# Selective scans in one kernel of four layers: x of the next task fetched a block ahead, five tiles for delta * x, other landing times

## The chip, the cores and the metric

The program runs on one NeuronCore of a Trainium2 chip. Its time is the device time of one execution in microseconds; the figure compared is the median over several runs. The profile is of one execution.

## The reference

Four layers follow each other on an input of 4 images of 64 x 64 points and 128 channels. Layers 0 and 1 are selective scans with projections, convolutions and norms around them; layer 2 is a gate over the edges to nine neighbours and layer 3 is attention in a 7 x 7 window. Nearly all of the time, and all that the change touches, lies in layers 0 and 1. Their core, here of layer 1 (256 channels, 16 states a channel, 4 directions; layer 0 has 128 channels):

```python
xs = jnp.stack([x0, x1, x0[..., ::-1], x1[..., ::-1]], axis=1)   # rows, columns, and both reversed
x_dbl = jnp.einsum('bkdl,kcd->bkcl', xs, x_proj_w)
dts, Bs, Cs = jnp.split(x_dbl, [R, R + N], axis=2)
dts = jnp.einsum('bkrl,kdr->bkdl', dts, dt_w)
delta = jax.nn.softplus(dts + dt_b[None, :, :, None])
A = -jnp.exp(A_log).reshape(K, DI, N)

def step(h, t):
    x_t, d_t, B_t, C_t = t
    h = jnp.exp(d_t[..., None] * A) * h + (d_t * x_t)[..., None] * B_t[:, :, None, :]
    return (h, jnp.einsum('bkdn,bkn->bkd', h, C_t))
...
ys = jnp.moveaxis(ys_l, 0, -1) + Ds.reshape(K, DI)[None, :, :, None] * xs
```

The sequence has 4096 steps.

## The kernel before

**Tasks, steps, units.** A task is one image, one layer and one tile of 128 channels: 4 tasks of layer 0 (tasks 0 to 3), then 8 of layer 1 (tasks 4 to 11, two for each image). The two tasks of one image share x and the projections of the first of them; in the code `t.first` names that first task. A task has 16 steps: 4 directions by 4 pieces of 1024 positions. A step has 16 units; a unit is 8 channels x 16 states = 128 rows by 1024 positions. So there are 12 x 256 = 3072 units, and `Scans.run` emits them in one loop over `u`. A group of 16 units is called a block here.

**One unit.** SP loads `dub`, the 8 rows of delta * x, each for its 16 states, from DRAM (`load`, 512 KB). POOL multiplies it by B into `dbu` (`times_b`). PE spreads three bfloat16 parts of delta (`dp`) over 128 rows into a PSUM tile `da`, and ACT takes the exponential of it in place (`decay`). DVE scans `da` and `dbu` into `da`, copies the last column to `state`, and multiplies by C into `hc` (`scan`). Every four units PE adds up the states with the constant `gather` (`add_up`). In iteration u the loop emits scan(u), times_b(u+3), decay(u+2) and load(u+6). There are 4 dub tiles, 3 dbu, 2 da.

**Preparation.** Each block needs a preparation (`prepare`), begun 22 units ahead (`AHEAD`): projection matmuls of x into `xd`, a store of it to `xdd` in DRAM, a delta projection from `xd` and `dtw`, softplus of it over ACT and POOL, the product delta * x on POOL (`low`), its store to DRAM (`dud`), three bfloat16 parts of delta (`parts`), loads of B and C repeated over channels (`repB`, `repC`), and 12 loads of `dp`. A second task of an image loads `xd` back from `xdd` instead of projecting. Each `yield` in `prepare` ends a piece. One unit of the loop is `rest` of its block: at rest 0 the old preparation is run to its end and the next one is started.

**x.** `fetch` loads the x of a task (`xc`, one tile for each 128 channels, single buffered) in 4 chunks of 512 KB a tile. It is called where the first step's preparation starts; the first chunk of each tile goes out at once, the others one a unit.

**The planner.** All instructions are put in order by hand when the program is built. `Plan` keeps an estimate of when PE, ACT and POOL are free; a piece is taken into a unit if it `fits`, that is if its start, not earlier than the time its data is taken to have landed, plus its usual cost, is before the end of the unit plus some slack. `LANDING`, `FOUR_LANDING` and `ROWS_LANDING` are those landing times. Stores are posted and issued when they are due. Where fewer than `rest - 2` pieces are out, a piece is taken without a look at the estimate.

**The side work.** Everything else of layers 0 and 1 (projections, convolutions, norms, the MLP) is cut into pieces as well and put between the units (`between`), paced by what is left until the next deadline. `last` holds the unit by which the side work that feeds a scan group must be out; past it, all of it is taken at once.

All engines work in order, and SP issues nearly all transfers. So an instruction that waits holds back what stands behind it on its engine: a projection of x on PE holds the decay products, a dub load on SP holds every later transfer.

Of the kernel before, what the change touches and what calls it, by code (L numbers as in the profile page):

```python
# [17 lines left out]
P = 128  # L18
# [26 lines left out]
class Consts:  # L45


    def __init__(self, tc, pool, d_gather, d_spread):
        nc = tc.nc

        self.gather = pool.tile([P, 4, 32], F32, name="gather")
        nc.sync.dma_start(out=self.gather, in_=d_gather)

        self.spread = pool.tile([96, 4, P], BF16, name="spread")
        with tc.tile_pool(name="spread32", bufs=1) as tmp:
            spread = tmp.tile([96, 4, P], F32, name="spread32")
            nc.sync.dma_start(out=spread, in_=d_spread)
            nc.vector.tensor_copy(self.spread, spread)
        self.ident = pool.tile([P, P], F32, name="ident")
        make_identity(nc, self.ident)  # L60
        self.ones128 = pool.tile([P, P], F32, name="ones128")
        nc.vector.memset(self.ones128, 1.0 / 128.0)
        self.ones256 = pool.tile([P, P], F32, name="ones256")
        nc.vector.memset(self.ones256, 1.0 / 256.0)
        self.cen128 = pool.tile([P, P], F32, name="cen128")
        nc.vector.tensor_sub(self.cen128, self.ident, self.ones128)
        self.cen256 = pool.tile([P, P], F32, name="cen256")
        nc.vector.tensor_sub(self.cen256, self.ident, self.ones256)
        self.neg256 = pool.tile([P, P], F32, name="neg256")
        nc.vector.memset(self.neg256, -1.0 / 256.0)  # L70
        self.eps = pool.tile([P, 1], F32, name="eps")
        nc.vector.memset(self.eps, EPS)

# [33 lines left out]
UNIT = 3.85  # L107
USUAL = dict(PE=2.1, ACT=0.7, TAB=3.3, POOL=1.3)
SLACK = dict(PE=1.2, ACT=2.2, POOL=3.0)
LANDING = 6.0  # L110
FOUR_LANDING = 12.0
ROWS_LANDING = 12.0


class Plan:
# [84 lines left out]
class ScanWeights:  # L200


    def __init__(self, tc, pool, layer, d_xp, d_dtw, d_av):
        nc = tc.nc
        self.layer, self.nct, self.rank = layer, TILES[layer], RANKS[layer]
        nct, rank = self.nct, self.rank
        self.xp = pool.tile([P, nct, ND, H], F32, name=f"xp{layer}")
        nc.sync.dma_start(out=self.xp, in_=d_xp)
        self.dtw = pool.tile([H + rank, ND, nct * P], F32, name=f"dtw{layer}")
        for i in range(HALVES):  # L210
            nc.sync.dma_start(out=self.dtw[i * H : i * H + rank], in_=d_dtw)
        n = ND * nct * NG
        av = pool.tile([P, n + 2 * ND * nct], F32, name=f"av{layer}")
        nc.sync.dma_start(out=av, in_=d_av)
        self.a = av[:, 0:n]
        nc.scalar.activation(self.a, self.a, AF.Exp)
        nc.vector.tensor_scalar_mul(self.a, self.a, -1.0)
        self.dtb = av[:, n : n + ND * nct].rearrange("p (k t) -> p k t", k=ND)
        ds = av[:, n + ND * nct :].rearrange("p (t k) -> p t k", t=nct)
        self.dsum = pool.tile([P, nct], F32, name=f"dsum{layer}")  # L220
        nc.vector.reduce_sum(self.dsum, ds, axis=AX.X)


class Task:


    def __init__(self, W, b, ct, first, xcd, yd):
        self.W, self.b, self.ct, self.xcd, self.yd = W, b, ct, xcd, yd
        self.first = first
        self.xc, self.xdd, self.prepared, self.states, self.y = [], {}, {}, {}, None  # L230
        self.steps = [
            (k, c) for k in range(ND) for c in (reversed(range(NSTEP)) if k >= 2 else range(NSTEP))
        ]
# [6 lines left out]
class Scans:  # L240
# [33 lines left out]
    def fetch(self, t):  # L274

        if t.first:
            t.xc = t.first.xc
            return
        t.xc = [self.pool.tile([P, L], F32, name=f"xc{i}", tag=f"xc{i}", bufs=1) for i in range(t.W.nct)]
        for c in range(NSTEP):  # L280
            for i, xc in enumerate(t.xc):
                cols = slice(c * TS, (c + 1) * TS)
                self.nc.sync.dma_start(out=xc[:, cols], in_=t.xcd[i][:, cols])
                yield

    def prepare(self, t, step):
# [8 lines left out]
        if t.first is None:  # L295
            xdd = t.xdd[step] = self.dram.tile(
                [rows, TS], F32, name="xdd", tag=f"xdd{W.layer}", bufs=(4, 2 * len(t.steps))[W.layer]
            )
            ps = self.bank()
            for ti in range(W.nct):  # L300
                for i in range(HALVES):
                    nc.tensor.matmul(
                        image(ps[i * H : (i + 1) * H, :]),
                        W.xp[:, ti, k, :],
                        self.view(t.xc[ti], k, c, i, HALVES),
                        start=ti == 0,
                        stop=ti == W.nct - 1,
                    )
            yield "ACT"
            nc.scalar.copy(xd, ps)  # L310

            def store_xd():
                for i in range(HALVES):
                    nc.sync.dma_start(out=xdd[:, half(i)], in_=xd[i * H : i * H + rows, :])

            post("prep", store_xd)
            ready = max(self.plan.done, self.plan.now) + LANDING
            yield "PE"
        else:
            xdd, ready = t.first.xdd[step], begin  # L320
            for i in range(HALVES):
                nc.sync.dma_start(out=xd[i * H : i * H + R, :], in_=xdd[0:R, half(i)])
            yield "PE", self.plan.now + LANDING
# [33 lines left out]
        nc.scalar.copy(parts[:, 0, :], delta)  # L357
        nc.gpsimd.tensor_mul(image(low), image(delta), self.view(t.xc[t.ct], k, c, 0, 1))
        yield "POOL"
        dud = out["du"] = self.dram.tile([P, TS], F32, name="dud", tag="dud", bufs=3)  # L360
        post("prep", lambda: nc.sync.dma_start(out=dud, in_=low))
        nc.gpsimd.tensor_sub(delta, delta, parts[:, 0, :])
# [24 lines left out]

    def load(self, u):
        t, step, jj, j, g = self.unit(u)
        dud = t.prepared[step]["du"]  # L390
        dub = self.live["dub", u] = self.tile("dub", 4)
        src = bass.AP(dud.tensor, dud.offset + 8 * g * TS, [[0, NS], [TS, 8], [1, TS]])
        self.nc.sync.dma_start(out=dub, in_=src)

# [53 lines left out]
    def add_up(self, u, i):  # L448

        for v in range(u - 3, u + 1):  # L450
            t, step, jj, j, g = self.unit(v)
            cols = self.half(i)
            self.nc.tensor.matmul(  # L453
                self.live["yps"][32 * j : 32 * j + 32, cols],
                self.C.gather[:, jj, :],
                self.live["hc", v][:, cols],
                start=False,
                stop=jj == 3,
            )
            if i == HALVES - 1:  # L460
                del self.live["hc", v]
# [15 lines left out]
    def run(self, between):  # L477

        total = NU * len(self.tasks)
        first = self.tasks[0]  # L480
        for _ in self.fetch(first):
            pass
        for _ in self.prepare(first, 0):
            pass
        self.plan.start()
        pieces, fetch = Lane(self.plan, iter(())), iter(())
        for u in range(-6, total):
            if u >= 0:
                self.scan(u)
            if u >= 2:  # L490
# [16 lines left out]
                self.plan.flush("prep", "rep")  # L507
            if rest == 0 and 0 < ahead < total // NG:
                n, step = divmod(ahead, NU // NG)
                if step == 0:  # L510
                    self.plan.flush("side")
                    fetch = self.fetch(self.tasks[n])
                    for _ in range(self.tasks[n].W.nct):
                        next(fetch, None)
                pieces = Lane(self.plan, self.prepare(self.tasks[n], step))
            next(fetch, None)
            while (pieces.count < rest - 2 or pieces.fits()) and pieces.step():
                pass
            if u >= 0:
                n, i = divmod(u, NU)  # L520
                if self.later:
                    self.later.pop(0)()
                between(n, i)
            if 0 <= u + 6 < total:
                self.load(u + 6)
        self.add_up(total - 1, 1)
        self.keep(total - 1)
        while self.later:
# [3 lines left out]
class Side:  # L532
# [218 lines left out]
    def norm(self, xs, out, then):  # L751
# [20 lines left out]
        ps = self.bank()  # L772
        for i, sq in enumerate(sqs):
            nc.tensor.matmul(
                ps, C.ones128 if len(xs) == 1 else C.ones256, sq, start=i == 0, stop=i == len(xs) - 1
            )
        yield "ACT"
        rs = sqs[0]
        nc.scalar.activation(rs, ps, AF.Ln, bias=C.eps)
        nc.scalar.activation(rs, rs, AF.Exp, scale=-0.5)  # L780
        yield "POOL"
        for d in ds:
# [255 lines left out]
def scan_layers(tc, C, nb, x_in, d0, s0, d1, s1, out):  # L1038

    nc = tc.nc  # L1040
    with ExitStack() as es:
# [17 lines left out]
                group.append(n)  # L1059
        scans = Scans(tc, C, pool, psum, dram, tasks, plan)  # L1060

        last = {g: group.index(g) * NU - AHEAD - 1 for g in range(1, len(groups))}
        last[len(groups)] = NU * len(tasks) - 16
        lane, current, credit = None, None, 0.0

# [703 lines left out]
def selectors():  # L1769

    gather = np.zeros((P, 4, 32), np.float32)
    for p in range(P):
        for jj in range(4):
            gather[p, jj, 8 * jj + p % 8] = 1.0
    spread = np.tile(np.transpose(gather, (2, 1, 0)), (3, 1, 1))
    return gather, np.ascontiguousarray(spread)


# [143 lines left out]
```

## Time and profile before

| | us |
|---|---|
| time of the runs: median (lowest to highest, 3 runs) | 14386.92 (14371.29 to 14389.15) |
| the profiled execution: its own time | 14397.46 |
| the profiled execution: its span, first to last instruction | 14395.7 |
| ahead of the first scan | 203.5 |
| first scan to the end of the last product | 11519.8 |
| rest of layer 1, layers 2 and 3 | 2672.4 |
| a scan on DVE, with and without a carried state | 2.350, 2.291 |
| the product by C on DVE, the state copy | 1.218, 0.158 |
| the product by B on POOL | 2.356 |
| the exponential on ACT | 1.089 |

The mean granted TensorE clock of this execution is 0.716; in the scans it is 0.68. The three largest busy shares of the span are DVE 87%, PE 72% and POOL 69%; the DMA queue of the program took 70.8% of 16 DMA engines. These are means over stages with different limits, so the stage of the scans has to be looked at by itself: its busy times, and, for each engine, what ended its waits. A line such as "DVE da L418 <- ACT da L408: 392.7, 312, 11.9" says that DVE's instructions at line 418 sat idle for 392.7 us in total, 312 times, 11.9 us at the longest, until ACT's instruction at line 408 released them. Line 98 is the planner's wrapper, through which all PE, ACT and POOL instructions pass, so there the tiles tell them apart: `mp` is the PSUM tile of the preparation, `ms` that of the side work.

The profile's page gives no landing times of these transfers. Where one is told below, it is worked out from the trace: from the issue to the last update of the transfer's semaphore before that semaphore's next use.

### The profile page before, as it was taken

The page shows a single profiled execution, that of the slowest core. Times are in us where ns is not written, and L with a number is a line of the kernel's source. Part 1 is how long each engine was busy: PE and PEld are TensorE (multiplying, and loading weights), DVE is VectorE, ACT ScalarE, POOL GpSimd, SP SyncE. Part 2 cuts the span into 40 slices and gives each one's busy share as a digit, 9 for nine tenths or more (in the row PEclk, how much of TensorE's full clock was granted, in tenths as well). Part 3 has the DMA queues.
Part 4 walks back from the last instruction along what each step waited for, and adds up shares of the span by engine and source line. Part 5 has one row for each costly group of instructions (what it writes and reads, how often), then busy time and mean ns, then how long its engine had stood idle before and what let it go on. Part 6 is the DMA issues. An engine that isn't in the chain of part 4 may idle for free. (4 is left out here: it accounts for less than half of the span.)

```text
span 14395.7 us, 123898 instructions
## 1 busy us (share of the span) xinstructions
PE 10393.2 (72%) x36216; PEld 2642.4 (18%) x36216; DVE 12507.0 (87%) x10488; ACT 7832.1 (54%) x9246; POOL 9888.4 (69%) x4606
## 2 busy tenths in 40 slices
PE   5777777777767777677776777767677766666999
PEld 1111111111111111111111111111111112113555
DVE  4998899989999999999998999999999954775666
ACT  3666456545655465555655555555555546553555
POOL 4777788778877788778887888888888853551000
PEclk7666666666677666677666777667776668777999
DMA  6888888888889888988889878778877841443000
GB/s 162 215 214 218 204 207 220 217 220 210 206 225 221 201 215 207 224 206 207 211 205 220 207 194 205 194 195 211 200 194 198 198 128 52 104 107 76 13 13 8
DMA packets 893467, 2567.49 MB, mean 178 GB/s; under 512 B 144375, under 2 KB 166143, under 8 KB 884599
## 3 DMA queue, kind: packets, MB, share of 16 engines
q1 hardware_dynamic: 892791, 2559.57, 70.8%
q8 instruction: 291, 4.77, 0.1%
q14 instruction: 385, 3.15, 0.1%
HBM read 2135.71 MB, written 272.37 MB: 167 GB/s over the span
## 5 line engine op out<-in xcount | busy, mean ns | idle before, releaser
L398 POOL TENSOR_TENSOR dbu<-dub,repB 128x1024 f32<-128x1024 f32 x3072 | 7195.6, 2356 | 1647.1 <-DVE da L418 859.1
L418 DVE TENSOR_TENSOR_SCAN da<-da,state,dbu 128x1024 f32<-128x1024 f32 x2304 | 5415.1, 2350 | 375.9 <-ACT da L408 287.9
L408 ACT ACTIVATE da<-da,av 128x1024 f32<-128x1024 f32 x3072 | 3342.0, 1089 | 3780.0 <-PE da L406 3736.2
L406 PE MATMUL da<-dp,spread 96*128 96x512 bf16 x6144 | 2603.8, 518 | 2953.2 <-DVE hc L430 2924.1
L430 DVE TENSOR_TENSOR hc<-da,repC 128x1024 f32<-128x1024 f32 x3072 | 3740.5, 1218 | 40.5 <-PE ms L98 0.5
L453 PE MATMUL yps<-hc,gather 128*32 128x512 f32 x12288 | 2376.5, 856 | 2.3 <-DVE hc L430 2.3
L418 DVE TENSOR_TENSOR_SCAN da<-da,dbu 128x1024 f32<-128x1024 f32 x768 | 1759.1, 2291 | 322.5 <-POOL dbu L398 212.4
L406 PEld LDWEIGHTS <-spread 96*128 96x128 bf16 x6144 | 474.3, 107 | 6513.8 <-DVE hc L430 4152.9
L98 ACT ACT_TABLE_LOAD x600 | 769.8, 1283 | 85.8 <-DMA xcd<-o 67.7
L98 PE MATMUL ms<-d,wts 128*128 128x512 f32 (+3 forms) x900 | 704.2, 905 | 141.8 <-POOL d L98 103.3
L98 POOL TENSOR_TENSOR delta<-delta,low 128x1024 f32<-128x1024 f32 x192 | 452.2, 2355 | 458.3 <-ACT low L98 457.9
L98 PE MATMUL mp<-xd,dtw 8*128 8x512 f32 (+1 forms) x768 | 674.5, 972 | 49.1 <-DMA xd<-xdd 31.2
L98 ACT CAST parts<-delta 128x1024 bf16<-128x1024 f32 x384 | 399.8, 1041 | 299.4 <-POOL delta L98 294.1
L446 PE MATMUL yps<-y,ident 128*128 128x512 f32 x576 | 528.9, 1013 | 2.9 <-ACT y L471 2.6
L453 PEld LDWEIGHTS yps<-hc,gather 128*32 128x32 f32 x12288 | 284.5, 128 | 1207.6 <-issue 1201.8
L98 POOL TENSOR_TENSOR low<-delta,xc 128x1024 f32<-128x1024 f32 x192 | 501.6, 2613 | 2.2
L1702 ACT ACTIVATE s<-s,nmax 128x512 f32<-128x512 f32 x512 | 366.1, 717 | 251.4 <-DVE nmax L1699 246.4
L1330 ACT ACTIVATE hid<-hid,relb 128x1024 f32<-128x1024 f32 x288 | 323.0, 1146 | 259.5 <-DVE hid L1325 259.3
L98 ACT ACTIVATE low<-mp,av 128x512 f32<-128x512 f32 x384 | 263.8, 687 | 365.6 <-PE mp L98 365.4
L1432 POOL TENSOR_TENSOR acc<-acc,part 128x1024 f32<-128x1024 f32 x120 | 315.1, 2633 | 211.7 <-DVE part L1426 154.6
L98 PE MATMUL ms<-pad,diag 96*32 96x504 f32 (+1 forms) x2304 | 423.7, 830 | 50.6 <-DMA pad<-xid 30.0
L1691 PE MATMUL sps<-k,q 32*128 32x512 f32 x1024 | 437.0, 652 | 21.2 <-DVE s L1698 21.2
(275 smaller groups left out, 11419.1 us busy)
## 6 DMA issues: line engine op xcount, KB each, us to landing
dub<-dud SPq DMA_DIRECT2D x3072, 512.0 KB
dp<-parts SPq DMA_DIRECT2D x2304, 64.0 KB
repB<-xdd SPq DMA_DIRECT2D x192, 512.0 KB
repC<-xdd SPq DMA_DIRECT2D x192, 512.0 KB
dud<-low SPq DMA_DIRECT2D x192, 512.0 KB
spread<-gd SPq DMA_DIRECT2D x72, 1024.0 KB
pad<-xid SPq DMA_DIRECT2D x192, 256.0 KB
szd<-o SPq DMA_DIRECT2D x96, 256.0 KB
```

The lines of the kernel that those rows point to most:

```text
L98: return call(*args, **kw)
L398: self.nc.gpsimd.tensor_mul(dbu, self.live.pop(("dub", u)), t.prepared[step]["B"])
L406: self.nc.tensor.matmul(da[:, cols], self.C.spread[:, jj, :], dp[:, j, cols], start=True, stop=True)
L408: self.nc.scalar.activation(da, da, AF.Exp, scale=t.W.a[:, at : at + 1])
L418: nc.vector.tensor_tensor_scan(da[:, way], da[:, way], dbu[:, way], 0.0 if step % NSTEP == 0 else t.states[step - 1][:, g : g + 1], ALU.mu ...
L430: nc.vector.tensor_mul(hc, da, t.prepared[step]["C"])
L446: self.nc.tensor.matmul(out, lhs, self.view(rhs, k, c, i, HALVES), start=True, stop=False)
L453: self.nc.tensor.matmul(self.live["yps"][32 * j : 32 * j + 32, cols], self.C.gather[:, jj, :], self.live["hc", v][:, cols], start=False, s ...
L1330: nc.scalar.activation(hid, hid, AF.Gelu, bias=self.relb[:, m, t : t + 1])
L1432: (nc.vector if alone and pair else nc.gpsimd).tensor_add(acc, acc, part)
L1691: nc.tensor.matmul(sps[:, h, :], q[ch, toks], k[ch, keys], start=True, stop=True)
L1702: nc.scalar.activation(s[:, i, :], s[:, i, :], AF.Exp, bias=nmax[:, h : h + 1], accum_out=total[:, h : h + 1],)
```

## The change

- `fetch` of the next task's x begins one block earlier: once the last preparation of the task before has emitted its product with the old x (`x_done`). One chunk goes out a unit. It flushes the side work's posted stores first. Where `x_done` isn't set in time, the fetch begins where it did.
- dub has five tiles and load(u+7) in place of four and load(u+6); the loop begins at -7. Posted stores of the preparation are flushed ahead of a block's first load.
- `LANDING` is 8 in place of 6, `ROWS_LANDING` 14 in place of 12.
- The projection matmuls of layer 1 (two tiles of x) are two pieces in place of one; pieces are forced up to `rest - 1` in place of `rest - 2`.
- Deadlines in `last` are 16 units sooner.
- Room in SBUF: `xp` and `dtw` of the two layers share one tile, loaded where the layer's first task is prepared; `gather` is a 56-column tile with four overlapping windows; `ones256` is gone and its factor moves into the scale of the logarithm.

```diff
@@ Consts
-        self.gather = pool.tile([P, 4, 32], F32, name="gather")
-        nc.sync.dma_start(out=self.gather, in_=d_gather)
+        gather = pool.tile([P, 56], F32, name="gather")
+        nc.sync.dma_start(out=gather, in_=d_gather)
+        self.gather = [gather[:, 24 - 8 * jj : 56 - 8 * jj] for jj in range(4)]
...
-        self.ones256 = pool.tile([P, P], F32, name="ones256")
-        nc.vector.memset(self.ones256, 1.0 / 256.0)
...
-LANDING = 6.0
+LANDING = 8.0
 FOUR_LANDING = 12.0
-ROWS_LANDING = 12.0
+ROWS_LANDING = 14.0
@@ ScanWeights
-        self.xp = pool.tile([P, nct, ND, H], F32, name=f"xp{layer}")
-        nc.sync.dma_start(out=self.xp, in_=d_xp)
-        self.dtw = pool.tile([H + rank, ND, nct * P], F32, name=f"dtw{layer}")
-        for i in range(HALVES):
-            nc.sync.dma_start(out=self.dtw[i * H : i * H + rank], in_=d_dtw)
+        self.nc, self.pool, self.d_xp, self.d_dtw = nc, pool, d_xp, d_dtw
...
+    def load(self):
+        nct, most = self.nct, max(TILES)
+        tile = self.pool.tile([P, most * ND * (H + P)], F32, name="xpdt", tag="xpdt", bufs=1)
+        self.xp = tile[:, 0 : nct * ND * H].rearrange("p (t k h) -> p t k h", t=nct, k=ND)
+        at = most * ND * H
+        self.dtw = tile[:, at : at + ND * nct * P].rearrange("p (k c) -> p k c", k=ND)
+        self.nc.sync.dma_start(out=self.xp, in_=self.d_xp)
+        for i in range(HALVES):
+            self.nc.sync.dma_start(out=self.dtw[i * H : i * H + self.rank], in_=self.d_dtw)
@@ Scans.fetch
         if t.first:
             t.xc = t.first.xc
             return
+        self.plan.flush("side")
@@ Scans.prepare
-            yield "ACT"
+                yield "PE" if ti + 1 < W.nct else "ACT"
             nc.scalar.copy(xd, ps)
...
         nc.gpsimd.tensor_mul(image(low), image(delta), self.view(t.xc[t.ct], k, c, 0, 1))
         yield "POOL"
+        t.x_done = step == len(t.steps) - 1
@@ Scans.load
         t, step, jj, j, g = self.unit(u)
+        if g == 0:
+            self.plan.flush("prep")
         dud = t.prepared[step]["du"]
-        dub = self.live["dub", u] = self.tile("dub", 4)
+        dub = self.live["dub", u] = self.tile("dub", 5)
@@ Scans.run
         first = self.tasks[0]
+        first.W.load()
...
-        for u in range(-6, total):
+        for u in range(-7, total):
...
-                if step == 0:
-                    self.plan.flush("side")
-                    fetch = self.fetch(self.tasks[n])
+                if step == 0 and self.tasks[n].W is not self.tasks[n - 1].W:
+                    self.tasks[n].W.load()
+                if step == 0 and fetched < n:
+                    fetch, fetched = self.fetch(self.tasks[n]), n
                     for _ in range(self.tasks[n].W.nct):
                         next(fetch, None)
                 pieces = Lane(self.plan, self.prepare(self.tasks[n], step))
+
+            n, step = divmod(ahead + 1, NU // NG)
+            if step == 0 and fetched < n < len(self.tasks) and self.tasks[n - 1].x_done:
+                fetch, fetched = self.fetch(self.tasks[n]), n
             next(fetch, None)
-            while (pieces.count < rest - 2 or pieces.fits()) and pieces.step():
+            while (pieces.count < rest - 1 or pieces.fits()) and pieces.step():
                 pass
...
-            if 0 <= u + 6 < total:
-                self.load(u + 6)
+            if 0 <= u + 7 < total:
+                self.load(u + 7)
@@ Side.norm
-                ps, C.ones128 if len(xs) == 1 else C.ones256, sq, start=i == 0, stop=i == len(xs) - 1
+                ps, C.ones128, sq, start=i == 0, stop=i == len(xs) - 1
...
-        nc.scalar.activation(rs, ps, AF.Ln, bias=C.eps)
+        nc.scalar.activation(rs, ps, AF.Ln, bias=C.eps, scale=1.0 / len(xs))
@@ scan_layers
-        last = {g: group.index(g) * NU - AHEAD - 1 for g in range(1, len(groups))}
+        last = {g: group.index(g) * NU - AHEAD - NG - 1 for g in range(1, len(groups))}
```

More of the change, by code (lines that the diff above doesn't have):

```diff
@@ L67, in __init__ @@
         self.cen256 = pool.tile([P, P], F32, name="cen256")
-        nc.vector.tensor_sub(self.cen256, self.ident, self.ones256)
         self.neg256 = pool.tile([P, P], F32, name="neg256")
         nc.vector.memset(self.neg256, -1.0 / 256.0)
+        nc.vector.tensor_add(self.cen256, self.ident, self.neg256)
         self.eps = pool.tile([P, 1], F32, name="eps")
@@ L229, in __init__ @@
         self.first = first
+        self.x_done = False
         self.xc, self.xdd, self.prepared, self.states, self.y = [], {}, {}, {}, None
@@ L454, in add_up @@
                 self.live["yps"][32 * j : 32 * j + 32, cols],
-                self.C.gather[:, jj, :],
+                self.C.gather[jj],
                 self.live["hc", v][:, cols],
@@ L485, in run @@
         self.plan.start()
-        pieces, fetch = Lane(self.plan, iter(())), iter(())
-        for u in range(-6, total):
+        pieces, fetch, fetched = Lane(self.plan, iter(())), iter(()), 0
+        for u in range(-7, total):
             if u >= 0:
@@ L1775, in selectors @@
     spread = np.tile(np.transpose(gather, (2, 1, 0)), (3, 1, 1))
+    gather = np.concatenate([gather[:, 3, :], np.zeros((P, 24), np.float32)], 1)
     return gather, np.ascontiguousarray(spread)
```

## The prediction

> **What bounds the kernel now.** I read the page first for the busy times and the slices, then one window from the first scan to the end of the last, then the waits of each engine inside it, then the timeline around single stalls.
>
> ```profile
> DVE  4998899989999999999998999999999954775666
> ...
> DMA  6888888888889888988889878778877841443000
> ```
> ```profile
> 203.50:11723.30 11519.80, 8226.40 (x25364) 1702.62 (x25364) 10888.92 (x8460) 6362.61 (x6667) 9292.30 (x4270) 0.68 0.83 208
> ```
>
> The reader is to see that VectorE is nearly full for 32 of 40 slices. The window's columns are its length, then busy time and count of PE, PEld, DVE, ACT and POOL, then clock, DMA share and GB/s. DVE is busy 10888.9 of 11519.8 us (94.5%), and 3072 units share the window: 3.75 us a unit, of which 3.54 are work. Nothing in the diff shortens a scan, a state copy or a product on DVE, so all that can be won here is DVE's idle time, 11519.8 - 10888.9 = 630.9 us. The other 203.5 us ahead and 2672.4 us behind hold no part of the change that matters.
>
> ```profile
> DVE da L418 <- ACT da L408: 392.7, 312, 11.9
> DVE da L418 <- POOL dbu L398: 291.2, 66, 187.1
> ```
> ```profile
> POOL dbu L398 <- DMA dub<-dud: 712.5, 293, 20.0
> ```
> ```profile
> PE mp L98 <- DMA xc<-xcd: 55.5, 7, 12.6
> PE ms L98 <- DMA pad<-ld: 50.2, 8, 9.8
> PE mp L98 <- DMA xd<-xdd: 31.2, 6, 11.8
> ...
> PE ms L98 <- DMA x<-yd: 17.2, 4, 6.3
> PE ms L98 <- DMA x<-in_x_dram: 14.7, 2, 7.7
> ```
> ```profile
> ACT L98 <- DMA xcd<-o: 67.7, 19, 11.9
> ACT sq L98 <- DMA xid<-sq: 37.9, 21, 6.5
> ```
>
> These are waits between 200 and 11730 us: who waited for whom, sum, times, longest. 187.1 us of the second line is the wait for the very first unit, so DVE's named idle time in the scans is 392.7 + 104.1 and some 10 of smaller lines, 506 us; the remaining 125 us are gaps under 150 ns. The engines in front of DVE in turn stand for transfers. I went through the scans with a gap over 150 ns and asked of each whether PE, ACT or POOL had waited for a transfer in the 3.5 us ahead of the gap or inside it: that holds for 262 of the 506 us. By transfer: dub 77.6 us (38 gaps), xc 51.3 (7), pad 40.0 (8), xd 30.7 (6), the side work's x 32.1 (7), stores that ACT waited for 29.4 (10). The other 244 us are ACT and PE being late without a transfer; the change does not touch their causes.
>
> **The x fetch.** The start of task 3 shows the case:
>
> ```profile
> 3061.83 0.29 PEld L98 LDWEIGHTS mp<-xc,xp 128*64 128x64 f32 x4 [13.54 <-DMA xc<-xcd]
> 3061.83 1.98 PE L98 MATMUL mp<-xc,xp 128*64 128x512 f32 x4 [12.63 <-DMA xc<-xcd]
> ...
> 3066.00 2.36 DVE L418 TENSOR_TENSOR_SCAN da<-da,state,dbu 128x1024 f32<-128x1024 f32 x1 [11.89 <-ACT da L408]
> ```
>
> The first projection is issued in the same unit as its chunk of x and stands on PE in front of the next decay product, behind which stand ACT's exponential and the scan. At the seven starts that fetch (tasks 1, 2, 3, 4, 6, 8, 10) DVE lost 11.89 + 6.67 + 11.89 + 6.43 + 7.74 + 7.28 + 4.92 = 56.8 us. After the change the first chunk goes out when the last product with the old x has been issued. The store of that product (dud) stands a median 26.9 us ahead of the next block's first dub issue in this trace, so the fetch starts some 6 units (23 us) before the block ends; by the semaphore updates an xc chunk lands in a median 8.5 us, at most 15.7. So the wait is gone at six starts. At task 4 it is replaced: the scan weights of layer 1 are now loaded there (3 transfers, an earlier such issue takes 0.33 to 0.43 us) directly ahead of the projection that needs them. The trace has them only at the start of the program; bounds are 0 and the 11.89 us of the worst x start. I take the 6.4 of this same start. **Gain 56.8 - 6.4 = 50 us**; bounds 45 and 57. The moved step issues the same 48 chunks on SP. Behind chunk 0 on SP stand the next dub loads: it waits for POOL to have read the old x, at most one sum and one product (2.36 + 2.61 = 5.0 us). A dub lands a median 4.7 us before it is used, and 3.75 more with the fifth tile, so this is hidden; uncovered it costs 7 x 5.0 = 35 us. I charge 5.
>
> **The fifth dub tile.** Load u+7 into five tiles waits for the same product (u+2) as load u+6 into four. So SP is held as before, but each load has a unit, 3.75 us, more. The 38 gaps lie in 26 clusters; cutting each cluster's sum by 3.6 us (a unit's work) leaves 14.9 of 77.6. **Gain 63 us**; bounds 0 (the transfers are bandwidth, and depth buys nothing) and 78. DMA share is 0.83 over the stage and 0.77 to 0.89 by task, so lateness comes in bursts, which depth covers: I stay near the upper end. The first load of a block now comes a unit sooner behind the store it reads: that store had landed at least 4.8 us before, so 1.0 us is left.
>
> [...] The trace has a median landing of 6.1 us, 10.3 at the ninetieth percentile and 19.7 at most, and the 293 waits above: I go by the trace.
>
> **Landing times.** The planner holds a piece until its transfer is due. Measured by semaphore updates: pad of the convolutions median 12.1 (ninetieth percentile 16.5) against a constant of 12; xcd stores 8.7, none under 7.0, against 6; xd 4.4 (6.2). Pieces go out once a unit, so 2 us more delay one by 2 us on average. Pad: 8 gaps x 2 = 16; side x: 7 x 2 = 14; stores: 10 x 2 = 20. xd is deterministic: ready 6 us after its issue fits at the second unit (3.85 + 1.2 + 3.85 covers 6 + 2.1), ready after 8 only at the third, so a whole unit: 6 x 3.75 = 22. **Sum 72**, of 132 that stand there; bounds 0 and 132. A later piece still can collide elsewhere, so I take 60.
>
> **What costs or gives nothing.** The split of the four projection matmuls into two pieces, and pieces forced a unit sooner (dud goes out a median 7.2 units ahead of its block's end, and the old rule forces it only 3 ahead, so few are forced): 0, bounds -10 and +15. The side work's deadline 16 units sooner: the last xcd stores of the four layer-1 groups come at units 753, 1192, 1612 and 2024 against new deadlines of 985, 1497, 2009 and 2521, so 232 to 497 units are to spare. Gather window, the removed constant, the scale inside the logarithm: same instructions, one 0.17 us memset less. Weights of layer 0 loaded at u=-7 instead of at 4.2 us: 3 issues of some 0.4 us ahead of an x fetch that waits for the side work's last store anyway.
>
> **Sum.** 50 - 5 + 63 + 60 = 168 us off the profiled execution's 14397.5 us (span 14395.7): 14229. The median of the runs, 14386.9, is 10.5 lower, which would give 14219. I say **14225**.
>
> **The rivals.**
> *Depth and landing give nothing* (0.17): dub lateness is bandwidth, and delayed pieces land on other units; x alone remains. For it: DMA share 0.9 in slices. Against: tasks 8 to 11 run at 0.77 to 0.81 and still show 3 to 5 us of gap a block at times. Time 14397 - 45 = 14350, faster by 0.3%.
> *No difference* (0.09): the stall of x returns as a later one, since chunks (512 KB a unit beside dub's 512 KB, 280 GB/s against 226 at best in any 400 us) now crowd the dp loads of the last block; 14360 to 14415. Against: the same crowding stood at the block's start before.
> *The change does not do what it says* is in this too: if the last product is issued only in the last unit, the fetch falls back to the old place.
> *Slower* (0.11): held pieces put the side work behind. Place: the last side group, whose final store comes at unit 3047 against a deadline of 3056, where all that is left is issued at once. Price: about 1.3 us of DVE idle a piece (a table load takes 1283 ns, an ACT piece 0.69 us). It decides from 168 / 1.3 = 130 pieces left, of 290; with 200 left the time is 14397 - 168 + 260 = 14490. Against: the pace is computed anew each unit from what is left, and credit lets several pieces go in one unit.
>
> **How the numbers follow.** Forecast 0.63: its own range is 14397 less 95 (x 45, half of dub's 60, a third of the landings' 60) to 262 (all that stands behind transfers), 14135 to 14302. A measurement here tells 0.2%, 29 us, from no change. Faster: forecast 0.63 and 0.17 of the first rival; same 0.09; slower 0.11. The range goes from 14110 (all 262, and 25 of the untouched 244) to 14375, which takes in the first rival and part of the second; what is left out is the slower case, the rest of the second and some 0.03 below.
>
> **What would show it.** Right: no PE wait for xc inside the scans save at task 4 (there for the weights); POOL's wait for dub well under 712 us, DVE's for POOL near 40 (without the first 187); PE waits for pad, xd and x and ACT waits for xcd and xid stores about half; DVE's busy time in the scans unchanged at 10889 and the stage near 11350 us; the 2672 us behind unchanged. Wrong: POOL still waits some 700 us for dub, or DVE's wait for ACT stays at 390, or grows in the last 60 units.

## The result, and the profile after

The changed kernel takes 14310.4 us (median of 4 runs, 14285.4 to 14319.5) against 14388.0 us before (4 runs): ratio 0.9946, 95% interval 0.9929 to 0.9963. That is 78 us less, where 163 were forecast. The profiled execution has a span of 14299.9 us, 95.8 less than before's; all but 0.6 of it is in the stage of the scans. (Lines of the kernel have moved by some ten: after the change, line 97 is the planner's wrapper, 410 the product by B, 420 the exponential, 430 the scan and 405 the load of dub; `xpdt` is the tile of scan weights that the two layers share.)

The window of the scans, after; columns as before (length, busy time and count of PE, PEld, DVE, ACT and POOL, clock, DMA share, GB/s):

```profile
202.70:11627.30 11424.60, 8187.62 (x25364) 1684.33 (x25364) 10879.78 (x8459) 6357.95 (x6665) 9285.10 (x4270) 0.69 0.85 210
```

The stage is 95.2 us shorter at nearly the same busy time of DVE (10879.8 against 10888.9), and 14299.9 - 11627.3 = 2672.6 us follow it, as before. So 86 of the 95 us are idle time of DVE, 544.8 us in place of 630.9. Lines picked from the waits of DVE, POOL, PE and ACT, after, from 200 to 11640 us, and from those of SP, from 200 to 11620 us:

```profile
DVE da L430 <- ACT da L420: 374.2, 309, 11.8
DVE da L430 <- POOL dbu L410: 232.8, 43, 186.3
```
```profile
POOL dbu L410 <- DMA dub<-dud: 367.5, 132, 18.3
```
```profile
PE ms L97 <- DMA pad<-ld: 35.8, 4, 11.8
PE ms L97 <- DMA x<-in_x_dram: 23.0, 2, 15.0
PE mp L97 <- DMA xpdt<-in_w_dram: 12.0, 1, 12.0
PE ms L97 <- DMA x<-yd: 11.9, 3, 4.6
...
PE mp L97 <- DMA xd<-xdd: 0.4, 1, 0.4
```
```profile
ACT L97 <- DMA xcd<-o: 100.0, 24, 11.0
```
```profile
SPq L405 <- DMA dud<-low: 128.9, 30, 14.4
```

The reader is to see that most of what was announced happened at its own place. PE no longer waits for xc, nor for xd (31.2 us before); POOL waits half as long for dub (712.5), and DVE for POOL 46.5 us without the first unit (104.1). But ACT's wait for the stores of the depthwise convolution went up from 67.7 to 100.0 us, PE's waits for the side work's x (31.9 us before, 34.9 after) were not halved, and DVE's wait for ACT only fell from 392.7 to 374.2. The last line is new: at 30 block starts SP stands at the load of dub until the store of delta * x (dud) that it reads has landed; before the change that was one wait of 0.7 us.

To compare kernels I sorted every gap of over 150 ns ahead of a scan by one rule: to dub where POOL ended it; else to the transfer for which PE or ACT had waited longest since the previous exponential; else to no transfer. (This counts all gaps that POOL ended, so dub stands at 112.0 us before, where the prediction's narrower rule gave 77.6.) All in us, from one profiled execution each:

| | all gaps | dub | xc | weights | xd | pad | side x | stores | no transfer |
|---|---|---|---|---|---|---|---|---|---|
| before | 511.4 | 112.0 | 51.3 | 0 | 14.2 | 38.5 | 32.9 | 40.7 | 213.9 |
| after | 425.7 | 47.2 | 0 | 11.0 | 0.7 | 36.6 | 32.6 | 85.9 | 201.3 |

"Side x" is the x that the side work loads. Gaps of under 150 ns and small kinds are in the first column alone. Where PE and ACT had both waited, the rule must choose: before the change some 18 us could stand under stores or under xd.

### The profile page after: what moved, and what is told of

It is laid out like the page before. It is cut to its first block, busy times and chain, and to the rows that moved or that the text cites. A ratio compares the mean times of both kernels' runs of the same rounds, so it can differ in the third digit from the quotient of the medians.

```text
span 14299.9 us, 124251 instructions
## 1 busy us (share of the span) xinstructions
PE 10354.0 (72%) x36216; PEld 2624.8 (18%) x36216; DVE 12498.6 (87%) x10487; ACT 7828.5 (55%) x9246; POOL 9880.8 (69%) x4606
## 5 line engine op out<-in xcount | busy, mean ns | idle before, releaser
L418 PE MATMUL da<-dp,spread 96*128 96x512 bf16 x6144 | 2568.6, 512 | 2952.1 <-DVE hc L442 2924.2
L97 PE MATMUL mp<-xd,xpdt 8*128 8x512 f32 (+1 forms) x768 | 656.9, 948 | 24.2 <-ACT delta L97 21.3
L1709 PE MATMUL sps<-k,q 32*128 32x512 f32 x1024 | 440.0, 656 | 21.2 <-DVE s L1716 21.2
L1343 DVE TENSOR_TENSOR hid<-cen,near 128x1024 f32<-128x1024 f32 x288 | 336.0, 1211 | 114.1 <-PE cen L1336 114.0
```

The costliest lines, as they stand in the source:

```text
L97: return call(*args, **kw)
L418: self.nc.tensor.matmul(da[:, cols], self.C.spread[:, jj, :], dp[:, j, cols], start=True, stop=True)
L1343: nc.vector.tensor_add(hid.rearrange("p i (r w) -> p (i r) w", w=HW), cen[pair].rearrange("p i (r w) -> p (i r) w", w=HW), self.near[m][s] ...
L1709: nc.tensor.matmul(sps[:, h, :], q[ch, toks], k[ch, keys], start=True, stop=True)
```

## The experiments

### Which part gives what: all eight combinations

The change has three main parts: the landing times, the fifth tile, the early fetch. Each was undone alone, and each was left alone; with the small edits kept throughout, that makes all eight combinations. The three edits, in the changed kernel:

```diff
# landing undone
-LANDING = 8.0
+LANDING = 6.0
-ROWS_LANDING = 14.0
+ROWS_LANDING = 12.0
# tile undone
-        dub = self.live["dub", u] = self.tile("dub", 5)
+        dub = self.live["dub", u] = self.tile("dub", 4)
-        for u in range(-7, total):
+        for u in range(-6, total):
-            if 0 <= u + 7 < total:
-                self.load(u + 7)
+            if 0 <= u + 6 < total:
+                self.load(u + 6)
# fetch undone
-            if step == 0 and fetched < n < len(self.tasks) and self.tasks[n - 1].x_done:
+            if False:
```

Landing undone (e1):

> The changed kernel with the two landing times put back to 6 and 12. Theory A (the landing times as a whole return about nothing, because what they save before pad and xd is lost before the stores of the depthwise convolution, which take 12 us or more from posting to landing): within 25 us of the changed kernel, ratio to before 0.993 to 0.997; PE waits for xd come back to some 30 us, ACT waits for xcd stores stay above 60 us. Theory B (8 in place of 6 is itself what moved pieces into the stores): faster than the changed kernel by 30 to 50 us, ratio 0.991 to 0.993, ACT waits for xcd back under 70 us. Theory C (as predicted, landing is worth 60): ratio 0.998 to 1.000.

Tile undone (e2):

> The changed kernel with four dub tiles and the load six units ahead. Theory D (the fifth tile is worth the 49 us that DVE's gaps behind dub lost, and does no harm): 45 to 55 us slower than the changed kernel, ratio 0.997 to 0.999, POOL waits for dub back above 600 us, ACT waits for xcd stores still near 100. Theory E (more dub loads in flight make the stores land later, so the tile takes back part of what it gives): median landing of the xcd stores back from 9.5 to 8.8 us, ACT waits for them back to 70 us or less, time within 25 us of the changed kernel, ratio 0.993 to 0.996.

Fetch undone (e4):

> The changed kernel with the x fetch begun where the preparation of the task's first step begins, as before. Theory: PE waits for xc come back at seven starts, 45 to 60 us of engine wait, DVE's gap there 45 to 55 us, in the place of 11 at task 4: 35 to 45 us slower than the changed kernel, ratio 0.996 to 0.998. Rival (the early chunks crowd out dub and the stores, so the early fetch gives part of it back): less than 20 us slower, with POOL's waits for dub under the changed kernel's 367 us and xcd stores' landing back under 9 us.

All three undone (e8), and each of them alone (e5, e6, e7):

> The changed kernel with old landing times, four dub tiles and the fetch at the old place: what is left is the shared weight tile with its load at task 4, the pieces forced a unit sooner, the split projection and the deadlines. Theory F (these small edits are worth nothing): ratio to before 0.999 to 1.001, DVE's gaps behind x stores, pad and xc as before the change, some 175 us in all. Theory G (they cost, and hide part of what the three main parts gain): 20 to 40 us slower than before, ratio 1.0015 to 1.003, with SP waits for the store of delta * x or DVE gaps behind the depthwise stores grown.

> Only the fifth dub tile of the three main parts. Theory F (the tile gains some 60 us behind dub and loses some 30 behind the stores that now land later): 20 to 40 us faster than with none, ratio about 0.997 to 0.9985; xcd stores' median landing 9.4 us or more. Rival (the tile costs nothing, and gives little as the last of three because the other two already take away the causes of late dubs): 55 to 70 us faster than with none, ratio 0.9955 to 0.9965.

> Only the early x fetch of the three main parts. Theory F (as the last of three it gave 5 us of time; its chunks crowd out dub, and with four tiles more so): within 20 us of none, ratio 0.998 to 1.000, the xc gap of some 55 us gone, dub's gaps 20 to 40 us above none's. Rival (what stands behind x, a pad load at task 3 and the weights at task 4, is all that eats it): 25 to 40 us faster than none, dub's gaps unchanged.

> Only the later landing times of the three main parts. As the last of three they gave 44 us. Theory F (they act on other waits than the two others): 35 to 60 us faster than none, ratio 0.9955 to 0.9975, PE waits for xd under 5 us. Rival (they only pay because the deeper dub makes transfers land later): under 20 us faster than none.

Measured, with the ratio to the kernel before on the same chip, and the gaps sorted as above:

| parts in | ratio (95% interval) | all gaps | dub | xc | weights | xd | pad | side x | stores |
|---|---|---|---|---|---|---|---|---|---|
| none (e8) | 1.0008 (0.9999 to 1.0018) | 526.1 | 90.8 | 61.9 | 0 | 19.4 | 49.6 | 32.1 | 40.6 |
| fetch (e6) | 1.0004 (0.9995 to 1.0013) | 522.0 | 142.4 | 0 | 5.0 | 14.7 | 47.5 | 33.4 | 47.1 |
| tile (e5) | 0.9985 (0.9974 to 0.9995) | 492.9 | 21.2 | 65.2 | 0 | 21.1 | 46.9 | 33.2 | 77.1 |
| landing (e7) | 0.9970 (0.9958 to 0.9981) | 471.6 | 91.2 | 58.2 | 2.3 | 0.4 | 18.0 | 27.7 | 55.7 |
| tile, fetch (e1) | 0.9975 (0.9966 to 0.9984) | 486.7 | 50.2 | 3.5 | 4.2 | 19.7 | 60.1 | 38.3 | 95.7 |
| landing, fetch (e2) | 0.9958 (0.9946 to 0.9971) | 467.3 | 156.1 | 0 | 11.1 | 1.3 | 2.5 | 28.4 | 59.2 |
| landing, tile (e4) | 0.9945 (0.9933 to 0.9958) | 444.0 | 19.3 | 60.6 | 3.1 | 1.2 | 26.0 | 27.4 | 85.1 |
| all, run again (e15) | 0.9946 (0.9932 to 0.9960) | 432.7 | 40.0 | 0 | 12.0 | 0.4 | 36.5 | 36.7 | 87.6 |

Against none, landing alone is 0.38% or 55 us, the tile 0.23% or 33 us, the fetch 0.04% or 6 us, less than these intervals can tell from nothing. They add up, 94 us, to what all of them are away from none (0.62%, 89 us). Theory A and B fall (landing does return something): undoing it costs 42 us, between A's range and C's. For the tile the time is E's: undoing it costs 0.12%, 17 us, with the stores' median landing from 9.5 back to 9.0 us; POOL's wait for dub comes back to 623 us, as D has it. Of e4's two, the rival holds in the time and in POOL's wait for dub (298.6 us), though the stores land in 9.4 us, hardly sooner. Theory F is right in the signs, but dub's gaps rose by 52 us with the early fetch where it had 20 to 40. The small edits (e8 against before) lie at +12 us, with an interval that takes in no change.

One rival is left untested for the landing times: the mean granted clock of the profiled executions is 0.715 to 0.717 with the old times (before, e8, e6, e5, e1) and 0.720 to 0.722 with the later ones (e7, e2, e4, e15, after). No run tells whether this is a cause of the shorter time or comes with it.

### Where the fetch's gain went

The fetch row is the clearest: xc 61.9 to 0, dub 90.8 to 142.4. In the 40 units around the seven starts (30 ahead of each, 10 behind) the gaps are 112.3 us without and 106.5 with it; of these dub has 10.2 and 65.1. Waits of DVE and POOL, first without (e8), then with the early fetch alone (e6):

```profile
DVE da L430 <- ACT da L420: 429.2, 319, 20.1
DVE da L430 <- POOL dbu L410: 276.1, 70, 186.0
```
```profile
DVE da L430 <- ACT da L420: 374.0, 331, 15.0
DVE da L430 <- POOL dbu L410: 327.6, 82, 185.9
```

DVE waits 55.2 us less for ACT and 51.5 more for POOL. The start of task 3 shows how. Timeline without the early fetch (e8):

```profile
3048.03 0.56 SPq L405 DMA_DIRECT2D dub<-dud  x1
3051.40 5.29 SPq L382 DMA_DIRECT2D dp<-parts  x3
3056.29 6.93 POOL L410 TENSOR_TENSOR dbu<-dub,repB 128x1024 f32<-128x1024 f32 x3 [17.67 <-DMA dub<-dud]
3056.73 1.08 SPq L292 DMA_DIRECT2D xc<-xcd  x2
...
3061.45 1.98 PE L97 MATMUL mp<-xc,xpdt 128*64 128x512 f32 x4 [20.52 <-DMA xc<-xcd]
...
3067.11 2.36 DVE L430 TENSOR_TENSOR_SCAN da<-da,state,dbu 128x1024 f32<-128x1024 f32 x1 [20.06 <-ACT da L420]
```

and with it (e6):

```profile
3026.41 3.39 SPq L681 DMA_DIRECT2D pad<-ld  x4
...
3027.83 1.98 PE L97 MATMUL mp<-xc,xpdt 128*64 128x512 f32 x4
...
3029.89 0.55 SPq L405 DMA_DIRECT2D dub<-dud  x1
...
3040.64 1.98 PE L97 MATMUL ms<-pad,wts 128*64 128x512 f32 x4 [10.84 <-DMA pad<-ld]
...
3048.75 2.34 POOL L410 TENSOR_TENSOR dbu<-dub,repB 128x1024 f32<-128x1024 f32 x1 [16.94 <-DMA dub<-dud]
...
3051.13 2.36 DVE L430 TENSOR_TENSOR_SCAN da<-da,state,dbu 128x1024 f32<-128x1024 f32 x1 [15.60 <-POOL dbu L410]
```

Both gaps are before the same unit, 749. Four loads of pad, 2.1 MB, go out at 3026 to 3030; the dub load behind them, issued at 3029.89, is there when POOL starts at 3048.75. Without the early fetch the four pad loads go out from 3034.40, and the same dub is as late (POOL waits 17.67 us for it). What held x there was SP's own queue. The transfers that SP issues in the scans take eight semaphores in turn, and in the trace each issue waits until the transfer eight issues earlier has landed. Between 3037 and 3058 us SP waits for these landings alone, 8.7 us for the pads and at last, until 3056.16, for that same dub; so x is issued at 3056.73. PE's wait for x was the last link of a chain that began with pad. With x there in time, the chain's other end, dub itself, holds DVE for 15.60 of the 20.06 us. In this stretch with the fetch (3000 to 3051 us) the DMA share is 0.96 at 232 GB/s.

At the other six starts no pad load stands ahead of x, and no such pair of timelines was made. What the traces have for all seven together: in those 40 units a dub lands in a mean 8.4 us without and 8.1 us with the early fetch, against 6.9 over all units in both. So late dubs are there in either kernel, and the early chunks did not make them later on average; without them, DVE stood for x meanwhile. With five tiles and the later landing times (e4 against e15) the 60.6 us of xc come back under four names: dub 21, pad 11, side x 9 and weights 9 us more.

### What the chunks and the single store tile cost

A chunk every four units after the first ones (e9), and two tiles in turn for the depthwise convolution's output (e10):

```diff
# e9 (`since` is the unit where the fetch began)
-        pieces, fetch, fetched = Lane(self.plan, iter(())), iter(()), 0
+        pieces, fetch, fetched, since = Lane(self.plan, iter(())), iter(()), 0, -99
...
-                fetch, fetched = self.fetch(self.tasks[n]), n
-            next(fetch, None)
+                fetch, fetched, since = self.fetch(self.tasks[n]), n, u
+            if u % 4 == 0 or u - since < self.tasks[fetched].W.nct:
+                next(fetch, None)
# e10, in depthwise
+            tag = ("o", "d0")[half]
...
-                yield "PE" if dx != 2 else self.when("TAB", "o")
+                yield "PE" if dx != 2 else self.when("TAB", tag)
-            o = self.tile("o")
+            o = self.tile(tag)
...
-            self.store("o", self.across(dst, i * n, n, 4 * half), o)
+            self.store(tag, self.across(dst, i * n, n, 4 * half), o)
```

> The changed kernel, with the early fetch spread: the first chunk of each tile of x a unit each as before, then one chunk every four units instead of every unit. Theory H (a chunk a unit beside a dub a unit is more than the DMA engines carry, and the dubs that come late of it are what ate the early fetch): DVE's gaps behind dub from 47 to 25 us or less, stores and pad no worse, 15 to 35 us faster than the changed kernel, ratio 0.9920 to 0.9937. Rival I (what counts is that the first chunk goes out at all, or the dubs are late for another cause): gaps behind dub stay above 40 us, time within 10 us of the changed kernel.

> The changed kernel, with the depthwise convolution's o in two tiles in turn (o and d0, which it does not use otherwise), so that the wait for a store has a whole chunk more. Theory J (the 86 us behind stores are the wait for the single buffer, and are lost to nothing else): ACT waits for xcd under 20 us, gaps behind stores under 20 us, 40 to 70 us faster than the changed kernel, ratio 0.9897 to 0.9920. Rival K (as with the longer hold, what is freed stands at the next thing, pad or side x): gaps behind stores gone, pad and side x up by half of it or more, under 30 us faster, ratio above 0.9925.

Before these, the single tile was kept and the store only counted as landed after 16 us (e3; `store(..., 16.0)` in place of `LANDING`):

> The changed kernel, with the depthwise convolution's stores of o counted as landed 16 us after posting in place of 8. Theory A (those 86 us of DVE gaps are pieces issued too early, and holding them is free): gaps behind the stores under 25 us, 45 to 70 us faster than the changed kernel, ratio 0.989 to 0.992. Rival (a held piece only lands on another unit, or the side work falls behind): ACT waits for xcd gone, but DVE's wait for ACT stays above 350 us, time within 20 us of the changed kernel.

Both of e9 and e10 with the weights of layer 1 loaded at the early fetch (e11, run again as e16), and that with the 3x3 convolutions' pad counted as landed after 20 us (e12, `self.halves(load, 20.0)` in `conv`):

> Both of these, and the weights of layer 1 loaded with the early fetch instead of at the step's start. If the parts add up: 25 (dub) + 55 (stores) + 11 (weights) = 90 us faster than the changed kernel, ratio about 0.988, no gap behind weights. If they only displace each other: 30 us or less, ratio above 0.992.

> The version with spread chunks, two store tiles and the early weights again: 20 to 60 us faster than the changed kernel beside it, ratio 0.990 to 0.9926.

> The one before, and the pad of the 3x3 convolutions counted as landed after 20 us instead of 14. If that is free: pad gaps from some 37 to under 10 us, 20 to 30 us faster than without. If the held pieces only land elsewhere: within 10 us.

| | ratio (95% interval) | all gaps | dub | weights | pad | side x | stores | no transfer |
|---|---|---|---|---|---|---|---|---|
| after | 0.9946 (0.9929 to 0.9963) | 425.7 | 47.2 | 11.0 | 36.6 | 32.6 | 85.9 | 201.3 |
| store counted 16 us (e3) | 0.9943 (0.9930 to 0.9957) | 433.0 | 57.3 | 0 | 28.9 | 66.8 | 71.8 | 200.7 |
| chunks spread (e9) | 0.9927 (0.9914 to 0.9939) | 423.0 | 28.1 | 9.5 | 31.1 | 37.1 | 97.7 | 208.3 |
| two store tiles (e10) | 0.9926 (0.9913 to 0.9940) | 422.9 | 88.7 | 10.2 | 48.7 | 45.3 | 0 | 215.0 |
| spread, two tiles, weights (e11) | 0.9912 (0.9899 to 0.9926) | 395.2 | 75.2 | 0 | 51.4 | 42.4 | 0 | 213.0 |
| the same again (e16) | 0.9919 (0.9905 to 0.9933) | 388.2 | 69.6 | 0 | 44.2 | 42.3 | 0 | 220.7 |
| and pad counted 20 us (e12) | 0.9946 (0.9933 to 0.9958) | 449.2 | 121.7 | 0 | 12.9 | 52.2 | 3.4 | 238.0 |

e9 takes dub's gaps from 47 to 28 us, near theory H's 25, but those behind stores go from 86 to 98, and the sum of all gaps is the same within 3 us in its one profiled execution; its median of 14289.9 us lies 20 below the changed kernel's, with overlapping intervals. e10 is the same story as the fetch: ACT's waits for xcd stores are gone, and dub takes half of what is freed, pad and side x a third. The time is rival K's; the place is not, as K had pad and side x up by half or more. Waits of DVE and POOL in e10:

```profile
DVE da L430 <- ACT da L420: 329.4, 296, 11.4
DVE da L430 <- POOL dbu L410: 270.3, 73, 182.7
```
```profile
POOL dbu L410 <- DMA dub<-dud: 417.5, 161, 18.3
```

Of 44.8 us less behind ACT, 41.1 come back behind POOL (270.3 - 182.7 against 232.8 - 186.3). e3 changed nothing in the time, and 71.8 us of gaps behind stores stayed. In the changed kernel a store takes, from ACT's end to its issue and from there to landing, a median 3.1 + 9.5 us (27 of 88 stores take over 16 together), and the planner lets a piece go up to some 6 us ahead of the time counted. So 16 is probably still too short; no run here tries a longer one. e12 shows the price of a count that is too long: pad's gaps go, dub's rise by 46 us and all gaps by 54.

e11 and e16 are the best version found: 38 us faster than the changed kernel beside it (14270.4 against 14308.0 us), between what adding up (ratio 0.988) and mere displacement (above 0.992) would give.

### Is it the amount of traffic?

B and C loaded for one step of four only (e13; it leaves out the rows of B and C of the other three), and a copy of 512 KB in DRAM more in each block (e14):

```diff
# e13, in repeat
+            if step % 4:
+                out["BC"[i]] = t.prepared[step - 1]["BC"[i]]
+                return
# e14, in load
+        if g == 2:
+            copy = self.dram.tile([P, TS], F32, name="copy", tag="copy", bufs=2)
+            self.nc.sync.dma_start(out=copy, in_=dud)
```

> The changed kernel, with B and C loaded only for one step of four and used for the other three (the rows of B and C of those steps are left out): 288 transfers of 512 KB less, 6% of the traffic; every engine does the same work. Theory L (the amount of traffic sets the waits): the gaps that stand behind transfers, 220 us, go down by half or more wherever they stand, 100 to 180 us faster than the changed kernel, ratio 0.982 to 0.988. Theory M (each wait has its own cause, such as a landing time or a single buffer): only dub's 47 us and some of the landings shrink, 20 to 60 us faster, ratio 0.990 to 0.993.

> The changed kernel with one copy of 512 KB from DRAM to DRAM more in each block, 192 in all, 4% more traffic, in front of nothing that waits for it. Theory L: 60 to 400 us slower than the changed kernel (a copy takes 2.4 us of the 16 engines at 213 GB/s, 192 of them 460 us, of which the idle share takes some), ratio 0.999 to 1.02, gaps behind dub and stores grown. Theory M: under 30 us slower.

> The changed kernel itself, as the reference of these runs: ratio 0.993 to 0.9963, about 0.9946.

| traffic | ratio (95% interval) | all gaps | dub | pad | stores | xcd store's median landing |
|---|---|---|---|---|---|---|
| 6% less (e13) | 0.9921 (0.9907 to 0.9934) | 391.8 | 39.7 | 33.3 | 45.9 | 8.9 us |
| as it is (e15) | 0.9946 (0.9932 to 0.9960) | 432.7 | 40.0 | 36.5 | 87.6 | 9.3 us |
| 4% more (e14) | 0.9963 (0.9950 to 0.9975) | 447.7 | 48.6 | 37.5 | 87.6 | 9.8 us |

37 us less and 21 us more: theory L falls, M is within its bounds. 6% less traffic takes half of the stores' gaps, but hardly any of dub's or pad's. So the sum of the traffic does not set those. That it is what stands in front of a load when it is issued is shown at the start of task 3 and argued for the rest.

The place does not decide it either. In the seven stretches of units with matmuls of the depthwise convolutions, 493 units in each kernel, the DMA share is 0.85 to 0.98 after the change. There DVE's gaps fell from 161 to 126 us (dub from 50 to 16 and xc from 32 to 0, but stores from 29 to 82); in the other 2579 units they fell from 345 to 295.

## Why the prediction was right and wrong

Of the 163 us forecast 78 came. Of the 85 that did not, the fetch has some 39 (45 forecast, 6 measured alone), the tile 30 (63 and 33), the landing times 5 (60 and 55) and the small edits 12 (0 and +12, not clear of nothing).

**What bounds the kernel: right.** DVE's work stayed at 10880 to 10889 us, the parts ahead and behind did not move, and 86 of the 95 us won in the profile were DVE's idle time.

**The landing times: right in the sum, in part by luck.** Forecast 60 us, alone 55. xd is as worked out (19.4 to 0.4 us, a whole unit later), but pad gave 32 where 16 were forecast, the side work's x 4 for 14, and the stores lost 15 where 20 were to be won. Some 14 us more came from gaps that stand in none of these columns, which the step left untouched. So the sum came out because errors of both signs met in it.

**The fifth tile: the mechanism right, the sum not.** "Cutting each cluster's sum by 3.6 us" was good: alone it takes dub's gaps from 90.8 to 21.2 us, 70 for the 63 forecast. The term that was missing is what the tile does to others. The step said "SP is held as before, but each load has a unit, 3.75 us, more", and costed no transfer behind it. With five tiles the stores of xcd land in a median 9.3 to 9.6 us in four kernels, with four in 8.8 to 9.0 in four (and in 8.7 before; but e3, with five, has 8.8), and the gaps behind stores go from 40.6 to 77.1 us with the tile alone. That leaves 33 us of 63. The landing is measured; that it is the store's own longer way through the queue and not also the units on which the pieces fall is not shown apart.

"SP is held as before" was wrong by itself, and with it "that store had landed at least 4.8 us before, so 1.0 us is left". In the ten kernels with five tiles whose SP waits I compared, SP stands 112 to 144 us in all, up to 15 us at a time, at the first load of a block until dud has landed; in those with four it is 0.6 to 1.6 us. No run shows how much of the tile's lost 30 us is this hold, nor why the store now lands so late for that load.

**The fetch: wrong.** Forecast 50 less 5 charged, measured 6 alone and 0 to 5 as the last of three. "So the wait is gone at six starts" came true to the letter, and the time did not follow. The step that failed is the price: that DVE would get back what it lost at the starts *to x*, with 5 us for all that stands behind. In its place the runs show that what stands next in the same units was late as well: around the starts dub's gaps alone rose by 55 us with four tiles (10.2 to 65.1). The charge of 5 was meant for the load held behind chunk 0 on SP, and was kept small because a dub lands a median 4.7 us before it is used; at the starts dubs take longer than the mean (8.1 to 8.4 us against 6.9). At task 3 the chain is seen whole; at the other starts only its sum.

The lines were also read too narrowly. At task 3 before the change the first chunk of x went out at 3053.31 us and took its usual 8.5 us; but inside PE's wait of 12.63 us POOL, too, had waited 4.86 and 1.96 us for dub, in the same answer of the trace. And the 6.43 us of task 4 are not x's: that gap ended at 4047.97 us, behind an exponential that stood after a wait of 6.45 us for a store of xid, while x cost 0.93 us there. As the same 6.4 was then taken for the weights, the sum of 50 did not change by it: that is luck.

**The weights at task 4.** 6.4 us taken; 11.0 and 12.0 in the changed kernel's two profiles, at the upper bound of 11.89, but 4.2 and 5.0 with the old landing times (e1, e6) and 16 to 17 in e13 and e14. **The small edits**, costed at 0, came out at +12 us with an interval from -1 to +26.

**The rivals.** "The stall of x returns as a later one" was the right mechanism for the fetch, at 0.09. The rival that had the x fetch as all that remains had it upside down. The side work did not fall behind: what follows the stage took 2672.6 us, as before.

**The lower bound of the tile**, that depth buys nothing, is out: the tile alone gave 33 us, at a median landing of 6.4 us for dub with 19.6 at most.

## What to carry to other kernels

A wait is put down to the transfer that came last; before it is priced, look whether the queue that issued this transfer was itself held, and by what, and what else in the same units is late but hidden behind this wait, or the stall will come back under the next name in the chain. Where one engine is the bound and many transfers share the queue, price an earlier or deeper prefetch by two terms, what it saves and what it does to the transfers that are issued behind it. And undo each part by itself: the three parts here gave 55, 33 and 6 us, and the one with the most convincing lines in the profile was the 6.

## What the runs showed of the hardware

Here one load's landing hung on what was issued just ahead of it: in the kernel with the early fetch alone dub takes a median 6.3 us, but 18.7 behind four pad loads of 2.1 MB. In the 51 us around it the DMA engines moved 232 GB/s with a share of 0.96, where the mean of the same execution's stage is 208 GB/s and 0.85. And 4% more traffic, in copies that nothing waits for, cost 0.17% of the time.
